# The depthwise convolution of a state-space block: products with pre-scaled weights on TensorE in place of multiply-adds on VectorE

## The chip, the cores and the metric

One core of one Trainium2 chip runs the whole program in one launch. The metric is device time in microseconds (us). The engines have queues of their own that run in order: TensorE (PE; its weight loads are shown as PEld), VectorE (DVE), ScalarE (ACT), GpSimd (POOL), and SyncE (SP), which issues nearly all DMAs. An instruction waits, with all that stands behind it on its queue, until what it reads is there and what it writes is free.

## The reference, cut to what matters

Layer 0 normalizes `x` (4 x 32 x 96 x 256, f32) in groups and runs two selective state-space blocks ("mamba") over it, one along the 96 time steps (way "t", sequences of length L = 96) and one along the 32 variables (way "d", L = 32). Each block computes, for a sequence of L tokens of 256 channels:

```python
xz = jnp.einsum('bld,ed->ble', x, in_w)
xi, z = jnp.split(xz, 2, axis=-1)                     # 512 channels each
xc = lax.conv_general_dilated(xi_nc, conv_w[:, None, :], (1,), [(D_CONV - 1, 0)],
                              feature_group_count=D_INNER)   # depthwise, causal, 4 taps
xc = jax.nn.silu(xc + conv_b[None, :, None]).transpose(0, 2, 1)
dbl = jnp.einsum('ble,fe->blf', xc, xproj_w)          # dt, B, C
# scan over l, 16 states per channel:
h = dA * h + dt_t[:, :, None] * B_t[:, None, :] * u_t[:, :, None]
y = jnp.einsum('bes,bs->be', h, C_t)
```

followed by a gate with silu(z) and an output product. Layer 1 is an additive attention over 3,072 tokens per batch entry and a graph-gated mixture of experts. The change touches only layer 0's convolution: for each channel, output l is the sum over j of `conv_w[3 - j] * xi[l - j]`, with nothing carried in from before the start of a sequence.

## The kernel before, in words

Layer 0 (`Layer0`) works in blocks of T = 384 tokens with 128 channels on the partitions, so a block has EC = 4 channel chunks e. Per batch entry there are 8 blocks of way t and 8 of way d. `run` writes the order by hand: t 0 to 7 of entry 0, then the first t block of entry 1, then d 0 to 7 of entry 0, and so on. The blocks 0 to 16 (`blk["lead"]`) run before anything else of the program does, since attention needs the finished rows of an entry; this is the stage that the change is in. From block 17 on, layer 0 runs beside attention, and ACT's large tanh sets the pace.

A block has a front (`front`: input product, convolution, xproj, time steps) and a back (`back`: decays, scans, products with C, gate), and the front of a block is issued beside the back of the one before. Both are lists of small jobs in 48 slots; `run` goes through the slots and issues, in each, first the back's scans and decays, then its inputs, outputs and sums, then the end of the block before, then the front's jobs. The order on PE, DVE, ACT and POOL is this order. SP's order is set by the framework's own scheduler.

The back walks 16 rounds of three slots (4 channel chunks x 4 groups of 4 states). A round has two scans of two states each. For each scan: ACT makes the decays `dA` (L470, two instructions, into one of two PSUM buffers that alternate), DVE makes `dB` (L483; every fourth one is made on POOL, L492), DVE scans (L503, `h`, four buffers), POOL multiplies `h` by C (L515), and PE sums the states with the identity as weights (L534, into `py`). After a chunk's 16 states DVE collects `py` (L541). Once per chunk PE makes the gate's product `pz` (L585).

The front's convolution, for chunk e, is `conv(e, s_mm, s_c0, s_c1, s_th, s_out)` at slots (13, 14, 15, 16, 18), (19, 20, 21, 22, 24), (22, 23, 24, 25, 27) and (25, 26, 27, 29, 30): PE makes `px`, two products of 128 x 128 weights with 384 columns (L296); ACT makes `acc = w[3] * px + bias` out of PSUM (L311, when the block before is a lead block); DVE adds three taps, each reading a shifted part of `px` (L302); ACT takes the tanh for the silu (L331); DVE finishes `xc` (L336). `px`, `pz`, `pd` (L349, xproj) and others share one PSUM buffer. In a round's terms, ACT's `acc` stands between the decays of one round and those of the next.

In way t POOL normalizes the block's input `xin` in slot 8 (L281); in way d ACT re-orders it into `xs`, so in a lead block the columns of one sequence are neighbours. The weights of the front (`self.wf`) are loaded at the start and again in slot 42 of the second-last block before the way changes (`fresh`), and `scale_front` rescales `xproj` on DVE there (L229). `uab` is a scratch tile that a front uses from slot 32 to 46.

Of the kernel before, what the change touches and what calls it, by code (L numbers as in the profile page):

```python
# [17 lines left out]
F32 = mybir.dt.float32  # L18
# [3 lines left out]
AF = mybir.ActivationFunctionType  # L22
# [4 lines left out]
P = 128  # L27
# [4 lines left out]
KC = C // P  # L32
# [101 lines left out]
class Layer0:  # L134
# [92 lines left out]
    def scale_front(self, t):  # L227
        nc, x = self.nc, t["xproj"]
        nc.vector.tensor_scalar(x, x, 0.5, None, ALU.mult)  # L229
        nc.vector.tensor_scalar(x[:, :, DR:DR + DS], x[:, :, DR:DR + DS], 0.5, None, ALU.mult)  # L230

    def scale_states(self, t):
        nc = self.nc
        nc.scalar.activation(t["A"], t["A"], AF.Exp)
        nc.vector.tensor_scalar(t["A"], t["A"], -1.0, None, ALU.mult)
        nc.vector.tensor_scalar(t["D"], t["D"], 0.5, None, ALU.mult)
# [5 lines left out]
    def front(self, blk, lead):  # L242
# [41 lines left out]
        elif alone:  # L284
            for k in range(KC):
                @at(11 + k)
                def _(k=k):
                    nc.scalar.copy(v["xs"][:, k, :].rearrange("p (s v) -> p s v", v=NV),
                                   v["xin"][:, k, :].rearrange("p (v s) -> p s v", s=ns))

        def conv(e, s_mm, s_c0, s_c1, s_th, s_out):
            @at(s_mm)
            def _():
                v["px"] = ps.tile([P, T], F32, tag="pp", name="px")
                for k in range(KC):
                    nc.tensor.matmul(v["px"], self.wf["in_x"][:, k, e * P:(e + 1) * P],  # L296
                                     blk["x"](k), start=(k == 0), stop=(k == KC - 1))

            def tap(j):
                a3 = v["acc"].rearrange("p (q l) -> p q l", l=L)  # L300
                p3 = v["px"].rearrange("p (q l) -> p q l", l=L)
                nc.vector.scalar_tensor_tensor(  # L302
                    a3[:, :, j:], p3[:, :, :L - j], self.wf["conv"][:, e, DCONV - 1 - j:DCONV - j],
                    a3[:, :, j:], ALU.mult, ALU.add)

            @at(s_c0)
            def _():
                v["acc"] = wk.tile([P, T], F32, tag="acc", name="acc", bufs=2)
                w, bias = self.wf["conv"][:, e, DCONV - 1:DCONV], self.wf["convb"][:, e:e + 1]
                if lead:  # L310
                    nc.scalar.activation(v["acc"], v["px"], AF.Identity, bias=bias, scale=w)  # L311
                else:
                    nc.vector.tensor_scalar(v["acc"], v["px"], w, bias, ALU.mult, ALU.add)
                    tap(1)

            @at(s_c1)
            def _():
                if lead:
                    tap(1)
                tap(2)  # L320
                tap(3)
                v["acc", e] = v["acc"]

            @at(s_th)
            def _():
                if alone:
                    blk["xc"][e] = self.ld.tile([P, T], F32, tag="xcl", name="xc", bufs=2 * EC)
                    xc = v["xt"] = self.ps_x.tile([P, 512], F32, tag="ex", name="xt")[:, :T]
                else:
                    xc = blk["xc"][e] = wk.tile([P, T], F32, tag="xc", name="xc", bufs=EC + 1)  # L330
                nc.scalar.activation(xc, v["acc", e], AF.Tanh, scale=0.5)  # L331

            @at(s_out)
            def _():
                xc = blk["xc"][e]
                nc.vector.scalar_tensor_tensor(xc, v["xt"] if alone else xc, 1.0, v["acc", e],  # L336
                                               ALU.add, ALU.mult)
# [410 lines left out]
    def run(self):  # L748

        order, NBLK = [], TOK // T
        for b in range(B):
            order += [(b, "t", i) for i in range(1 if b else 0, NBLK)]
            if b + 1 < B:
                order.append((b + 1, "t", 0))
            order += [(b, "d", i) for i in range(NBLK)]
        blocks = [{"b": b, "way": w, "i": i, "L": S if w == "t" else NV, "lead": n <= 2 * NBLK}
                  for n, (b, w, i) in enumerate(order)]

        FRONT, STATES = ("in_x", "conv", "convb", "xproj", "dt", "dtb"), ("A", "D", "in_z")

        def states_weights(blk):
            blk["w"] = {**self.weights(blk["way"], ("A", "D"), 2), **self.weights(blk["way"], ("in_z",))}
            self.scale_states(blk["w"])

        first = blocks[0]
        self.wf = self.weights(first["way"], FRONT)
        self.scale_front(self.wf)
        states_weights(first)  # L770

        def alone(*parts):
            for slot in range(48):
                fs = [f for part in parts for f in part.get(slot, [])]
                for f in fs:
                    f()
                if fs:
                    yield None
                    yield None

        yield from alone(self.front(first, True))
        left, ending = ({}, {}), {}
        rows = []
        for n, blk in enumerate(blocks):
            then = blocks[n + 1] if n + 1 < len(blocks) else None
            old = blocks[n - 1] if n else None

            fresh = then and n + 2 < len(blocks) and blocks[n + 2]["way"] != then["way"]
            if old is None or old["way"] != blk["way"]:
                if old and old["lead"] and not blk["lead"]:  # L790
                    self.dctx.close()
                    self.dA = self.decay_places(False)
                for t in self.dA:
                    for c0 in range(0, SB * T if blk["lead"] else T, T):
                        self.nc.vector.memset(
                            t[:, c0:c0 + T].rearrange("p (q l) -> p q l", l=blk["L"])[:, :, 0:1], 0.0)
            for name in ("bB", "bC"):
                for j in range(self.before(blk, name)):
                    if not left[1]:
                        self.broadcast(blk, name, j)  # L800

            breaks = then and (then["way"], then["i"]) == ("d", 0) and then["b"] == blk["b"]
            jobs, later = self.back(blk, None if breaks else then)
            ahead = self.front(then, blk["lead"]) if then and not breaks else {}
            for slot in range(48):
                self.slot = slot
                for f in left[0].get(slot, []) + jobs[0].get(slot, []):
                    f()
                yield None
                for part in (left[1], jobs[1], ending, ahead):  # L810
                    for f in part.get(slot, []):
                        f()
                if slot == 42 and old and "rows" in old:
                    rows = self.rows_keys(old)
                if rows:
                    rows.pop(0)()
                if slot == 12:
                    if old is None or old["way"] != blk["way"]:
                        blk["wo"] = self.weights(blk["way"], ("out",))
                        w = blk["wo"]["out"]  # L820
                        self.nc.vector.tensor_scalar(w, w, 0.5, None, ALU.mult)
                    else:
                        blk["wo"] = old["wo"]
                if slot == 42 and then:
                    if then["way"] == blk["way"]:
                        then["w"] = blk["w"]
                    else:
                        states_weights(then)
                    if fresh:
                        self.wf = self.weights(blocks[n + 2]["way"], FRONT)  # L830
                        self.scale_front(self.wf)
                if self.beside:
                    self.beside(slot, blk["way"] == "d" and blk["i"] >= min(PARTS))
                done = (old["b"], old["i"]) if old and slot == 11 and old["way"] == "d" else None
                if done == (0, NBLK - 1):
                    self.lctx.close()
                yield done
            left, ending = later, self.end(blk, bool(then and then["lead"]))
            if breaks:
                halves = 0  # L840
                for _ in chain(alone(*left, ending), alone(self.front(then, False))):
                    halves += 1
                    yield None
                left, ending = ({}, {}), {}
                for _ in range(-halves % (2 * NK_ATT)):
                    yield None
        yield from alone(*left, ending)
        yield blocks[-1]["b"], blocks[-1]["i"]
        yield None
# [1561 lines left out]
```

## Time and profile before

| | us |
|---|---|
| median of 3 runs | 14,503.21 (14,501.98 to 14,504.32) |
| the profiled execution, its own time | 14,508.64 |
| its span | 14,506.8 |
| PE, DVE, ACT, POOL busy in the span | 11,322 / 10,474 / 12,279 / 9,081 |

In the lead stage the profile's groups are: L302, the taps, 216 instructions of 0.58 to 0.61 us; L503, the scans, 1.75 us each, 32 per block; L483 0.95 us; L470 0.57 to 0.58 us; L515 1.8 us. One product in f32 shows as two matmul records. Times in the timeline count from the start of the span. In brackets stands how long an engine was idle before an instruction, and what released it.

### The profile page before, as it was taken

To read this page: it belongs to the slowest core of one execution; us is meant where nothing else is said; L and a number is where in the kernel's file an instruction comes from. 1 tells how busy PE (TensorE), PEld (TensorE's weight loads), DVE (VectorE), ACT (ScalarE), POOL (GpSimd) and SP (SyncE) were. 2 spreads that over 40 slices of the span, in tenths; PEclk is the share of its full clock that TensorE was granted. 3 is DMA by queue.
4 is the path that set the end of the run, shared out by engine and by line. 5 is a ranking of instruction groups with operands and counts; after the bars stand their busy time and mean duration, and the time that the engine had idled before them with its cause. 6 is when DMAs were issued, how large, how long until landed. Compare 5 with 4: busy or idle time off the path is not lost.

```text
span 14506.8 us, 224766 instructions
## 1 busy us (share of the span) xinstructions
PE 11322.4 (78%) x86704; PEld 5143.5 (35%) x86704; DVE 10473.8 (72%) x15217; ACT 12278.6 (85%) x9676; POOL 9080.5 (63%) x7108
## 2 busy tenths in 40 slices
PE   5777767777777777778887677788887788888888
PEld 2333322222232333333333233333333334443566
DVE  7888987787777877777777777757776785332376
ACT  4555569999999899999998899999999999999522
POOL 5777777777777667767776677747764003653373
PEclk8989978888888889989998899999989999999999
DMA  6778864445545444455554444435543100110233
GB/s 216 237 236 241 248 188 148 148 150 153 150 151 153 148 148 154 150 149 157 156 154 146 148 149 152 156 107 152 155 151 110 39 22 17 12 18 15 61 102 125
DMA packets 1199839, 1984.19 MB, mean 137 GB/s; under 512 B 418596, under 2 KB 646436, under 8 KB 1193636
## 3 DMA queue, kind: packets, MB, share of 16 engines
q1 hardware_dynamic: 1168036, 1963.77, 44.1%
q0 software_dynamic: 30720, 5.96, 0.9%
q8 instruction: 682, 11.17, 0.3%
q14 instruction: 401, 3.28, 0.1%
HBM read 1859.14 MB, written 110.18 MB: 136 GB/s over the span
## 4 chain that ended last, share of the span: by engine, by line


## 5 line engine op out<-in xcount | busy, mean ns | idle before, releaser
L1047 ACT ACTIVATE th<-krep,qsel 128x3072 f32<-128x3072 f32 x3072 | 8658.0, 2850 | 284.4 <-PE pe L1020 273.8
L1020 PE MATMUL pe<-th,wa_blk 128*32 128x384 f32 x49152 | 4933.7, 529 | 932.2 <-ACT pr L1115 691.0
L515 POOL TENSOR_TENSOR h<-h,bC 128x768 f32<-128x768 f32 x2048 | 3765.3, 1840 | 2769.4 <-DVE h L508 2198.2
L508 DVE TENSOR_TENSOR_SCAN h<-dA,dB 128x384 f32<-128x384 f32 x3008 | 2706.5, 941 | 895.9 <-ACT dA L470 673.8
L1020 PEld LDWEIGHTS pe<-th,wa_blk 128*32 128x32 f32 x49152 | 1468.5, 115 | 3408.8 <-issue 1877.1
L483 DVE TENSOR_TENSOR dB<-bB,dtu 128x768 f32<-128x768 f32 x1912 | 1809.9, 947 | 97.0 <-DMA bB<-bc 45.9
L522 POOL TENSOR_TENSOR h<-h 128x768 f32<-128x768 f32 x752 | 1413.5, 1880 | 53.6
L1133 PE MATMUL pv<-xn,pT 128*32 128x257 f32 x18432 | 1156.6, 401 | 216.7 <-DVE pT L1126 215.4
L470 ACT ACTIVATE dA<-dt,t_A 128x380 f32<-128x380 f32 x2048 | 1121.2, 571 | 230.2 <-DVE h L508 162.6
L534 PE MATMUL py<-h,ident 128*128 128x384 f32 x2176 | 930.0, 558 | 478.5 <-POOL h L515 370.4
L470 ACT ACTIVATE dA<-dt,d_A 128x372 f32<-128x372 f32 x2048 | 1107.2, 564 | 139.3 <-DVE h L508 91.8
L503 DVE TENSOR_TENSOR_SCAN h<-dA,dB 128x768 f32<-128x768 f32 x544 | 947.7, 1751 | 127.3 <-ACT dA L470 81.3
L1192 POOL TENSOR_SCALAR sf<-sel,f 128x32 f32<-128x32 f32 x384 | 137.3, 384 | 1239.3 <-ACT f L1188 1238.8
L1133 PEld LDWEIGHTS pv<-xn,pT 128*32 128x32 f32 x18432 | 598.4, 115 | 851.1 <-DVE pT L1126 373.7
L1108 DVE TENSOR_REDUCE nb<-pe 128x1 f32<-128x768 f32 x384 | 364.2, 948 | 729.0 <-PE pe L1020 697.1
L523 POOL TENSOR_TENSOR h<-h 128x384 f32<-128x384 f32 x752 | 790.4, 1051 | 59.0
L524 POOL TENSOR_TENSOR y<-y,h 128x384 f32<-128x384 f32 x752 | 777.1, 1033 | 59.0
L534 PEld LDWEIGHTS py<-h,ident 128*128 128x128 f32 x2176 | 420.2, 209 | 941.0 <-POOL h L515 583.5
L1124 PE MATMUL ptw<-ident,pr 128*128 128x128 f32 x2304 | 459.2, 314 | 306.4 <-DVE pT L1126 128.1
L1126 DVE COPY pT<-ptw 128x512 f32<-128x512 f32 (+1 forms) x768 | 417.6, 544 | 327.3 <-PE ptw L1124 315.4
L1276 POOL DMA_INDIRECT gd<-tab_a,di x480 | 498.3, 1038 | 159.2 <-issue 156.7
L1124 PEld LDWEIGHTS ptw<-ident,pr 128*128 128x128 f32 x2304 | 295.7, 159 | 770.9 <-issue 281.3
(329 smaller groups left out, 15071.9 us busy)
## 6 DMA issues: line engine op xcount, KB each, us to landing
bB<-bc SPq DMA_DIRECT2D x2048, 384.0 KB
bC<-bc SPq DMA_DIRECT2D x2048, 384.0 KB
x<-x SPq DMA_DIRECT2D x321, 128.0 KB
all<-kept SPq DMA_DIRECT2D x40, 1024.0 KB
kept<-ko SPq DMA_DIRECT2D x43, 512.0 KB
xt<-xn2T SPq DMA_DIRECT2D x41, 512.0 KB
qsel<-xn2T SPq DMA_DIRECT2D x75, 256.0 KB
kept<-eo SPq DMA_DIRECT2D x150, 128.0 KB
```

The lines of the kernel that those rows point to most:

```text
L470: nc.scalar.activation(inner(dA[:, s * T:(s + 1) * T] if alone else self.dA[s][:, :T]), inner(blk["dt"][:, e, :]), AF.Exp, scale=blk["w"][ ...
L483: nc.vector.tensor_tensor(dB, blk["bB"].pop(j), z["dtu"].unsqueeze(1).to_broadcast([P, SB, T]), ALU.mult)
L503: nc.vector.tensor_tensor_scan(flat(h), dA[:, :SB * T], flat(dB), 0.0, ALU.mult, ALU.add)
L508: nc.vector.tensor_tensor_scan(h[:, s, :], self.dA[s][:, :T], dB[:, s, :], 0.0, ALU.mult, ALU.add)
L515: nc.gpsimd.tensor_tensor(h, h, blk["bC"].pop(j), ALU.mult)
L522: nc.gpsimd.tensor_tensor(h0, h0, h1, ALU.add)
L523: nc.gpsimd.tensor_tensor(h0[:, 0, :], h0[:, 0, :], h0[:, 1, :], ALU.add)
L524: nc.gpsimd.tensor_tensor(y[e], y[e], h0[:, 0, :], ALU.add)
L534: nc.tensor.matmul(z["py"], self.ident, h[:, s, :], start=(i == 0), stop=(i == DS - 1))
L1020: nc.tensor.matmul(pe[q * QU:(q + 1) * QU, j, :KQ // 2], self.wa[:, k, :], th[:, c0:c0 + KQ // 2], start=(k == 0), stop=(k == NK - 1))
L1047: nc.scalar.activation(th, s["krep"], AF.Tanh, bias=s["qsel"][:, col:col + 1])
L1133: nc.tensor.matmul(pv[q * QU:(q + 1) * QU, :C + 1], pT[:, i, q * QU:(q + 1) * QU], s["xn"][:, q * NK + i, :], start=(i == 0), stop=(i == N ...
```

## The change

The convolution is linear in the input product, so the four taps can be put into the weights: `in_x4[:, j]` is `in_x` with each output channel multiplied by that channel's tap j. A convolution is then eight products, four taps times two chunks of 128 input channels, accumulated in one PSUM tile. The product of shift j writes the outputs from j on of each sequence and reads the inputs up to L - j, so its columns are 384 - 4j in way t (4 sequences of 96) and 384 - 12j in way d (12 of 32). ACT then only adds the bias, and DVE has no taps. `taps_load` brings `conv_w` flat to all 128 partitions (128 x 2,048 numbers, in the place of `uab`), `taps_make` makes `in_x4` with four DVE products of 128 x 1,024. This happens once in the prologue for way t, and for way d with the load in slot 47 of block 7 and the products in slot 6 of block 8. The fronts of blocks 0 to 16 take this way (`folded`); the front of block 17 and all later ones keep the old one. Taps and products of one convolution stay at the same slots.

```diff
+    def taps_load(self, t, way):
+        row = self.wide("taps")[:, :DI * DCONV]
+        flat = self.a[way]["conv_w"].rearrange("d k -> (d k)")
+        self.nc.sync.dma_start(row, flat.unsqueeze(0).to_broadcast([P, DI * DCONV]))
+        self.taps = t, row.rearrange("p (d k) -> p k d", k=DCONV)
+
+    def taps_make(self):
+        (t, row), self.taps = self.taps, None
+        t["in_x4"] = self.ld.tile([P, DCONV, KC, DI], F32, tag="inx4", name="inx4", bufs=1)
+        for j in range(DCONV):
+            self.nc.vector.tensor_tensor(t["in_x4"][:, j], t["in_x"],
+                                         row[:, j].unsqueeze(1).to_broadcast([P, KC, DI]), ALU.mult)
...
+        def folded():
+            return lead and "in_x4" in self.wf
...
                 v["px"] = ps.tile([P, T], F32, tag="pp", name="px")
+                if folded():
+                    parts = lambda t: t.rearrange("p (q l) -> p q l", l=L)
+                    for j in range(DCONV):
+                        for k in range(KC):
+                            nc.tensor.matmul(parts(v["px"])[:, :, j:],
+                                             self.wf["in_x4"][:, DCONV - 1 - j, k, e * P:(e + 1) * P],
+                                             parts(blk["x"](k))[:, :, :L - j],
+                                             start=(j == 0 and k == 0),
+                                             stop=(j == DCONV - 1 and k == KC - 1))
+                    return
...
-                if lead:
+                if folded():
+                    nc.scalar.activation(v["acc"], v["px"], AF.Identity, bias=bias)
+                elif lead:
                     nc.scalar.activation(v["acc"], v["px"], AF.Identity, bias=bias, scale=w)
...
-                if lead:
-                    tap(1)
-                tap(2)
-                tap(3)
+                for j in () if folded() else (1, 2, 3) if lead else (2, 3):
+                    tap(j)
...
         self.scale_front(self.wf)
+        self.taps_load(self.wf, first["way"])
+        self.taps_make()
...
+                if slot == 47 and fresh and blk["lead"] and blocks[n + 2]["lead"]:
+                    self.taps_load(self.wf, blocks[n + 2]["way"])
+                if slot == 6 and self.taps:
+                    self.taps_make()
```

## The prediction

> **What bounds the kernel now.** I read the page's busy shares, then the busy time in stretches of 100 us, because the change lives in the first stage alone: 17 blocks between 110 and 1,950 us of a 14,507 us span. Columns: stretch, length, then busy us and instruction count of PE, PEld, DVE, ACT, POOL, then the granted clock, the DMA share and GB/s. A t-block stretch and a d-block stretch:
>
> ```profile
> 560.00:660.00 100.00, 70.55 (x170) 33.35 (x171) 85.31 (x80) 51.86 (x94) 77.89 (x50) 0.90 0.79 243
> 1360.00:1460.00 100.00, 73.40 (x219) 38.43 (x219) 89.37 (x90) 60.06 (x119) 79.16 (x50) 0.94 0.82 241
> ```
>
> DVE is busiest (85 to 89%), and that is what the change relieves. But ACT, half idle, and PE are queues that run in order, so I asked next who waits for whom in the stage (waited us, times, longest):
>
> ```profile
> ACT acc L311 <- PE px L296: 214.2, 68, 9.3
> ...
> DVE h L503 <- ACT dA L470: 80.3, 85, 7.0
> ```
>
> ACT already stands at the convolution's first operation until PE has `px`, in nearly every one of the 72 convolutions, 3.1 us each. Behind it on ACT stand the decays `dA` of the next two scans, and DVE's longest loss is for `dA`. Last, the timeline of one convolution, the first of a d-block (start, duration, engine, operation, count, and the idle time before it):
>
> ```profile
> 1461.28 1.45 PE L296 MATMUL px<-xs,d_in_x 128*128 128x384 f32 x4
> 1462.59 1.76 DVE L503 TENSOR_TENSOR_SCAN h<-dA,dB 128x768 f32<-128x768 f32 x1
> 1462.77 0.67 ACT L311 ACTIVATE acc<-px,d_convb,d_conv 128x384 f32<-128x384 f32 x1 [3.14 <-PE px L296]
> 1463.34 2.27 ACT L470 ACTIVATE dA<-dt,d_A 128x372 f32<-128x372 f32 x4
> 1464.26 0.59 DVE L541 SCALAR_TENSOR_TENSOR y<-xc,d_D,py 128x384 f32<-128x384 f32 x1
> 1464.77 0.95 DVE L483 TENSOR_TENSOR dB<-bB,dtu 128x768 f32<-128x768 f32 x1
> 1465.00 1.53 PE L534 MATMUL py<-h,ident 128*128 128x384 f32 x4 [2.27 <-DVE y L541]
> 1465.63 1.84 DVE L302 SCALAR_TENSOR_TENSOR acc<-px,d_conv,acc 128x372 f32<-128x372 f32 x3
> 1466.26 1.81 POOL L492 TENSOR_TENSOR dB<-bB,dtus 128x768 f32<-128x768 f32 x1
> 1467.39 3.39 DVE L503 TENSOR_TENSOR_SCAN h<-dA,dB 128x768 f32<-128x768 f32 x2
> ```
>
> Each f32 product of 384 columns leaves two records, so x4 is two products. The chain reads: `px` done 1462.73, `acc` 1463.4, first `dA` pair 1464.5. DVE reaches its scan at 1467.39, 2.9 us after that pair: this is the slack that the longer `px` may use, and 1.84 us of it is the taps that go.
>
> **The change, part by part.**
>
> *Removed.* Three taps per convolution, 0.58 to 0.61 us each (mean by row), 1.84 to 1.90 us together. 17 fronts of four convolutions are folded: one alone in the prologue, eight of way t and eight of way d beside other blocks. The front of block 17 keeps the old path. In-stage that is 64 x 1.85 = 118 us of DVE.
>
> *Added on PE.* `px` becomes 16 records instead of 4. Records follow each other at 0.32 us (the 12-record row of 4.19 us, and 1.45 us for four with the last one's tail). For t the widths are 384, 380, 376, 372, so 16 x 0.315 = 5.04 us; for d 384, 372, 360, 348, so 4.9 us. With the tail 5.2 and 5.05, against 1.45. The shifted outputs are runs of 95 down to 29 elements; TensorE writing such runs into PSUM is not in this trace. Bounds: 0.315 us a record if runs cost nothing, and 2.92/4 = 0.73 us from the worst pattern shown, a moving operand read at a 48-byte step:
>
> ```profile
> 3324.39 2.92 PE L296 MATMUL px<-xin,d_in_x 128*128 128x384 f32 x4
> ```
>
> I take 0.315: runs of 29 and more neighbours are nearer to the plain rows than to single elements. The Trainium skill, SBUF — State Buffer, section "Door 1: The DMA port swizzle", speaks against the change here: it says that any non-contiguous access to PSUM slows matmuls significantly. It gives no factor; if the 12 shifted records went at the row's 0.73, `px` would take 10 us, 5 more per convolution, and the sum below would be about 320 us higher. No row of before can show it.
>
> *ACT.* `acc` stays, without the per-partition scale: 0.67 us now, 0.57 by the row of L383 (bias alone). I leave out that 0.1.
>
> *A d-block, put back together from the rows* (PE, ACT, DVE, POOL each in order). `px` 1461.28 to 1466.3; `acc` to 1466.95; first `dA` pair 1468.1; scan 1468.15, against 1467.39: +0.8 although the taps are gone. Behind `px` on PE stand the products that sum `h` (1465.00 in the rows, now 1466.2), then the gate product `pz`, which no longer waits for the taps and stays near its time. The next three convolutions come one per three slots, and there PE is the bound: between two `px` lie two sums of 1.28 us, so 5.05 + 2.56 = 7.6 us per round, where the rounds now take 7.2, 6.4 and 8.2 us. Carried on with the same durations, `px` starts at 1474.9, 1482.4, 1489.9 (now 1474.31, 1480.51, 1486.62), and the scan after the fourth at 1496.8 instead of 1494.3: +2.5 us. DVE has nothing left to give back, for it waits for `dA` in each round.
>
> *A t-block.* Here the first `px` has no slack, since PE gets to it late (POOL is behind after normalizing `xin`) and DVE stands at the tap for `acc`:
>
> ```profile
> 688.08 1.60 PE L296 MATMUL px<-xin,t_in_x 128*128 128x384 f32 x4
> ...
> 689.72 0.67 ACT L311 ACTIVATE acc<-px,t_convb,t_conv 128x384 f32<-128x384 f32 x1 [8.99 <-PE px L296]
> ...
> 690.42 1.90 DVE L302 SCALAR_TENSOR_TENSOR acc<-px,t_conv,acc 128x380 f32<-128x380 f32 x3 [0.62 <-ACT acc L311]
> 692.24 3.40 DVE L503 TENSOR_TENSOR_SCAN h<-dA,dB 128x768 f32<-128x768 f32 x2
> ```
>
> `px` to 693.25, `acc` to 693.95, `dA` 695.15, scan 695.15 against 692.24: +2.9. Then `px` at 701.9, 709.55, 717.2 (now 699.15, 705.35, 711.52), the following scans at 708.95, 716.55, 724.2 (now 704.66, 711.09, 719.27): +4.9 after the fourth. PE gets a little back, because it stays warm where it now runs a sum and `pz` at 2.90 us for four records: `pd` ends +4.7 late. I take +4.7.
>
> Blocks: 8 x 4.7 + 8 x 2.5 = +58 us. Afterwards every engine stands equally late and the rest of a block repeats the same pattern (the t-blocks' first scans lie 107.6 to 109.6 us apart), so nothing returns. Attention starts only after the stage, so the end moves by the same.
>
> *Prologue.* The taps of all 128 partitions are 128 x 8 KB = 1.05 MB, queued on SP among the loads of `xs`; at 262 GB/s (first 60 us) +4.0. Four products of 1,024 elements on DVE at L483's rate (0.95 us for 768, so 1.24) are 5.0 us, from 65.4 to 70.4, before PE can start, now 66.92: +3.4 (reading the taps at a step of four is not shown: up to twice that, +8.4). The chain of four convolutions and `pd` takes 25.5 us now (66.92 to 92.4); new: the first `px` half cold, 7.6, then three of 5.04, four `acc` of 0.67, tanh 0.5, xc 0.55, `pd` 2.75: 29.2, +3.7. Together +11.
>
> *Change of weights before the d blocks.* Another four products on DVE in block 8: +5 (to +10). Its 1.05 MB wait on SP for `uab`, read last in slot 46, and have seven slots, 15 us, to land: nothing, or some us if the broadcasts queued behind it on SP come late; their three and four buffers cover 10 us. And one gain: the program's SP queue now has the load of `d_xproj` eight broadcasts earlier. DVE stood 8.48 us for it at 975.10. I take -8.5 (bounds -8.5 and 0).
>
> Sum: 58 + 11 + 5 - 8.5 = +65 us. The profiled execution took 14,508.6 us, 5.4 above the median of three; against its own time that is 14,573, against the median 14,568.
>
> **The rivals.**
>
> *DVE's relief counts in full, the kernel gets faster.* For it: DVE is the busiest engine, and the row of DVE waiting for `dA` (80 us) is small. Then -118 + 11 + 5 - 8.5 = -110 us, 14,393. It needs ACT to pass `px` without delaying `dA`: it decides where `px` is below about 4.6 us in the three rounds (7.3 us, their mean now, less 2.56 + 0.1) and below 4.3 us in a d-block's first. Mine is 5.05, not far, so a half gain is possible; against it stand ACT's 68 waits.
>
> *Same.* If only the first convolution of each t-block lost (2.9 x 8 = 23) and the rest evened out: +23 + 7.5, about +30 us or less, which lies at the edge of 0.2% (29 us), what a measurement of this kernel can tell from none.
>
> *Shifted outputs are slow.* With 0.73 us a record: +65 + 64 x 5 = +385 us, 14,890.
>
> **How the numbers follow.** Slower as worked 0.70, its own range +30 to +130 us; slow shifted outputs 0.06; same 0.13; faster 0.11, mostly as half the gain. So slower 0.76, same 0.13, faster 0.11. The range leaves out the full gain and the slow outputs: 14,480 to 14,640.
>
> **What would show it.** Right: `px` groups of 16 records in about 5.1 us; ACT's wait for `px` near 214 + 64 x 3 = 400 us and more; DVE's wait for `dA` up from 80 to 200 us or more; DVE's share in 160 to 1,900 us down from 86 to about 79%; block distances of 113 us (t) and 110 (d). Wrong: `dA` waits unchanged and block distances near 101 us (the rival), or records of 0.6 us and over.

## The result and the profile after

The changed kernel takes 14,582.66 us (median of five runs, 14,576.89 to 14,586.24); the kernel before, run beside it, 14,501.98. The ratio is 1.0056, 95% interval 1.0044 to 1.0067: 81 us slower, where +65 was forecast. The profiled execution has a span of 14,584.4 us, 77.6 more than before.

Of these, 75 arise in the lead stage. From the first scan of one block to the first of the next, in the profiled execution of each kernel:

| us | before | after | |
|---|---|---|---|
| first scan of block 0 | 112.0 | 122.8 | +10.8 |
| blocks 0 to 6 (t), mean | 108.9 | 114.2 | +5.3 each |
| block 7 (t, last) | 115.0 | 112.8 | -2.2 |
| block 8 (first beside a d front) | 115.3 | 127.6 | +12.3 |
| block 9 | 115.8 | 118.0 | +2.2 |
| blocks 10 to 14 (d), mean | 107.35 | 109.9 | +2.6 each |
| block 15 | 108.0 | 110.2 | +2.2 |
| first scan of block 16 | 1,865.3 | 1,940.5 | +75.2 |
| from there to the end of the span | 12,641.5 | 12,643.9 | +2.4 |

The last row is the same work in every kernel here, and varies between 12,608 and 12,648 us over all the traces of this case: a total says less than the stage.

The same two stretches of the lead stage as in the prediction, with the same columns (stretch, length, busy us and count of PE, PEld, DVE, ACT, POOL, granted clock, DMA share, GB/s):

```profile
560.00:660.00 100.00, 78.82 (x221) 41.23 (x220) 75.27 (x64) 42.91 (x77) 77.25 (x49) 0.95 0.70 227
1360.00:1460.00 100.00, 82.14 (x253) 47.01 (x252) 81.65 (x79) 56.36 (x112) 75.46 (x47) 0.93 0.81 237
```

DVE did get its relief (85 to 75, 89 to 82). PE took the work on (71 to 79, 73 to 82), and no engine is above 83%: the stage has become one of waiting. Which wait, the view of waits between 112 and 1,935 us tells (us, times, longest):

```profile
ACT acc L339 <- PE px L317: 409.7, 64, 13.1
DVE h L531 <- ACT dA L498: 254.2, 145, 7.4
```

These two were 214 and 80 us. DVE lost 118 us of taps and waits 174 us longer for the decays. One stretch of the timeline shows how: rounds 4 to 7 of a t-block, counted from 0 (start, duration, engine, operation, count, and the idle time before it):

```profile
724.56 5.24 PE L317 MATMUL px<-xin,inx 128*128 128x384 f32 x16
...
729.84 0.58 ACT L339 ACTIVATE acc<-px,t_convb 128x384 f32<-128x384 f32 x1 [11.43 <-PE px L317]
730.32 2.30 ACT L498 ACTIVATE dA<-dt,t_A 128x380 f32<-128x380 f32 x4
...
731.59 3.40 DVE L531 TENSOR_TENSOR_SCAN h<-dA,dB 128x768 f32<-128x768 f32 x2 [5.36 <-ACT dA L498]
...
738.52 5.24 PE L317 MATMUL px<-xin,inx 128*128 128x384 f32 x16
...
743.60 2.74 PE L562 MATMUL py<-h,ident 128*128 128x384 f32 x8
...
743.80 0.58 ACT L339 ACTIVATE acc<-px,t_convb 128x384 f32<-128x384 f32 x1 [7.58 <-PE px L317]
744.28 2.30 ACT L498 ACTIVATE dA<-dt,t_A 128x380 f32<-128x380 f32 x4
...
745.56 3.40 DVE L531 TENSOR_TENSOR_SCAN h<-dA,dB 128x768 f32<-128x768 f32 x2 [3.26 <-ACT dA L498]
...
746.18 5.24 PE L317 MATMUL px<-xin,inx 128*128 128x384 f32 x16
```

ACT had nothing to do for 11.43 us, yet the decays `dA` of the next scans, which need nothing from `px`, stand behind `acc` on its queue; DVE in turn stands 5.36 us for them. From the second `px` on, PE goes `px` 5.24, sums 2.74, `px` 5.24, and so on (the rows overlap a little): 7.66 us from one `px` to the next. That is the round that the prediction built, 7.6 us.

The records of `px`, with their minimum, median and maximum in ns (a record overlaps the next one; 16 take 5.24 us in way t and 5.09 in way d):

```profile
L317 PE MATMUL px<-xin,inx x576: 473/482/977, 72.8 to 986.5; 128*128 128x384 f32 x48, 128*128 128x380 f32 x48, 128*128 128x376 f32 x48, 128*128 128x372 f32 x48
L317 PE MATMUL px<-xs,inx x512: 453/476/1008, 1073.1 to 1889.9; 128*128 128x384 f32 x43, 128*128 128x360 f32 x43, 128*128 128x348 f32 x43, 128*128 128x372 f32 x42
```

Before, with 384 columns in every record, the median was 486 ns. Writing the shifted outputs, in runs of 93 to 95 (t) and 29 to 31 (d) elements, cost nothing that these rows show.

Last the scaling of the weights, first in the prologue, then in block 8 (timeline):

```profile
64.58 9.44 POOL L296 TENSOR_SCALAR xin<-xin,gm,gr 128x384 f32<-128x384 f32 x2 [64.14 <-DVE t_xproj L229]
...
64.73 7.92 DVE L244 TENSOR_TENSOR inx<-t_in_x,taps 128x1024 f32<-128x1024 f32 x4
...
72.80 8.01 PE L317 MATMUL px<-xin,inx 128*128 128x384 f32 x16 [8.87 <-DVE inx L244]
...
1046.99 8.93 DVE L244 TENSOR_TENSOR inx<-d_in_x,taps 128x1024 f32<-128x1024 f32 x4
...
1048.79 10.13 SPq L461 DMA_DIRECT2D bB<-bc  x2
...
1055.83 1.76 DVE L531 TENSOR_TENSOR_SCAN h<-dA,dB 128x768 f32<-128x768 f32 x1
...
1064.61 5.64 SPq L280 DMA_DIRECT2D xin<-xt  x2
...
1072.22 0.85 ACT L303 COPY xs<-xin 128x384 f32<-128x384 f32 x1 [10.13 <-DMA xin<-xt]
```

Each product takes 1.95 to 3.23 us, not the 1.24 assumed, and POOL's two normalisations beside them take 9.44 us where they took 3.35. In block 8 the scans stand for 8.9 us: round 1 takes 14.5 us in place of 5.7. SP's queue, in order, holds a broadcast for 10.13 us, since its buffer comes free late, and the load of the next `xin` comes behind it; ACT waits 10.13 us for that. Most of this last wait is not new, for before the change ACT stood at the same place:

```profile
1018.67 0.86 ACT L288 COPY xs<-xin 128x384 f32<-128x384 f32 x1 [7.96 <-DMA xin<-xt]
```

The round that holds this wait grew only from 11.4 to 12.6 us.

### The profile page after: what moved, and what is told of

Same layout as the page of the kernel before. It is cut to its first block, busy times and chain, and to the rows that moved or that the text cites. A ratio compares the mean times of both kernels' runs of the same rounds, so it can differ in the third digit from the quotient of the medians.

```text
span 14584.4 us, 226136 instructions
## 1 busy us (share of the span) xinstructions
PE 11529.2 (79%) x87520; PEld 5304.1 (36%) x87520; DVE 10372.5 (71%) x15021; ACT 12267.6 (84%) x9676; POOL 9082.2 (62%) x7108
## 4 chain that ended last, share of the span: by engine, by line
ACT 40%; PE 27%; DVE 18%; issue 7%; POOL 5%; DMA 2%; SPq 1%; DVEq 0%; another core or an unknown queue 0%; POOLq 0%; ACTq 0%
ACT th L1081 28%; PE pe L1054 9%; ACT dA L498 6%; PE pv L1167 4%; DVE h L536 4%; DVE h L531 3%; PE px L317 2%; DVE dB L511 2%; POOL h L543 2%; PE po L1963 2%; PE py L562 2%; PE ph L1955 1%; ACT pr L1149 1%; PE pa L1711 1%; PE pz L613 1%
## 5 line engine op out<-in xcount | busy, mean ns | idle before, releaser
L562 PE MATMUL py<-h,ident 128*128 128x384 f32 x2176 | 891.7, 540 | 396.6 <-POOL h L543 357.4
```

The lines of the kernel that those rows point to most:

```text
L562: nc.tensor.matmul(z["py"], self.ident, h[:, s, :], start=(i == 0), stop=(i == DS - 1))
```

## The experiments

Theory: the loss is a matter of order. `px` is long, `acc` waits for it at the head of ACT's queue, the decays wait behind `acc`, and DVE's freed time becomes waiting. Rivals: DVE's taps were hidden all along; PE has simply become the bound; the loss lies in the scaling. The kernel before was measured again beside these runs; it took 14,482.88 us beside the first four, 14,495.43 beside the next two and 14,474.31 beside the last two, and each ratio and difference below goes by its own. The changed kernel was not run again, so what a run gains on it is the difference of two such differences. Block times come from one profiled execution of each kernel.

**The short product: what the taps' removal is worth without PE's price.** Only the products of shift 0 are made.

```diff
-                    for j in range(DCONV):
+                    for j in (0,):
...
-                                             stop=(j == DCONV - 1 and k == KC - 1))
+                                             stop=(k == KC - 1))
```

> The changed kernel with the products of shift 0 alone: px is 4 records as before, DVE has no taps, the loading and scaling of the weights stays. It leaves out three of the four taps of the convolution in the first 17 fronts. It asks what DVE's relief is worth when nothing is paid for it on PE. Theory (the long px, which holds up the decays on ACT, ate the relief): with px at 1.45 us the rounds of the convolutions fall from 7.3 to about 5.4 us, some 6 to 7 us per block, so about -90 to -110 us against before, minus and plus nothing for the prologue and the second scaling (+10, -8): 14,390 to 14,420 us. Rival (DVE's taps hid behind the wait for dA already, so nothing was to be had): within 25 us of before, 14,480 to 14,530.

14,441.53 us, ratio 0.9973 (0.9963 to 0.9983): 41 us faster, between the two. The t-blocks take 105.15 us and the d-blocks 104.2, so the full relief of 7.4 us per block is worth 3.8 and 3.2. Rounds 6 to 8, where three convolutions follow each other, shorten from 21.9 to 17.7 us, but then 0.7 us (0.4 in way d) goes in round 10 and, in way d, 1.0 in round 2. In round 10 ACT stands at `dbl` until PE has `pd`, and the decays of the next scan stand behind `dbl`. In the timeline:

```profile
1460.39 0.47 ACT L384 COPY dbl<-pd 48x384 f32<-48x384 f32 x1 [4.79 <-PE pd L377]
...
1462.03 1.76 DVE L531 TENSOR_TENSOR_SCAN h<-dA,dB 128x768 f32<-128x768 f32 x1 [1.40 <-ACT dA L498]
```

So the rival of the prediction, a gain of 110 us from DVE's relief, was not there to be had in this order: with `px` no longer at all than before the gain is 41 us, scaling included. Some 6 us more may hide in block 7, which takes 111.8 us: DVE stands 8.0 us there for `d_xproj`, as it did before the change (8.5) and does in no run with a long `px`.

**The long product with the taps kept.** The kernel before, with 16 records of the changed shapes from the unscaled weights (so it computes something else); no taps loaded, nothing scaled.

```diff
+                if lead and alone:
+                    parts = lambda t: t.rearrange("p (q l) -> p q l", l=L)
+                    for j in range(DCONV):
+                        for k in range(KC):
+                            nc.tensor.matmul(parts(v["px"])[:, :, j:],
+                                             self.wf["in_x"][:, k, e * P:(e + 1) * P],
...
```

> The kernel before with px as 16 records (the shifted shapes, unscaled weights) and the taps left on DVE; the convolution's output is another one, since px is the sum of shifted products. It asks what the long px costs alone, with no scaling and no relief. Theory (with px at 5.1 us the rounds are set by PE and by ACT's wait, and DVE's 1.85 us per convolution lie beside them): nearly the same loss in the blocks as the change has, +60 to +100 us with the prologue, 14,560 to 14,600. Rival (the relief counts in full and the long px costs what it ate, some 118 + 60 us): +160 to +200 us, 14,660 to 14,700.

14,596.28 us, ratio 1.0082 (1.0065 to 1.0099): 113 us slower, more than the 60 to 100 that I expected (the 14,560 to 14,600 named there count from 14,502) and far from the rival's 160 to 200. Blocks: 115.7 (t), 112.3 (d); the first scan comes 16.6 us later than before, since in the prologue the taps and the long `px` stand one behind the other. Against the changed kernel's 114.2 and 109.9, taking the taps away under the long `px` is worth 1.5 and 2.4 us per block, a fifth and a third of DVE's 7.4. The waits say where the taps went:

```profile
DVE acc L312 <- ACT acc L321: 106.8, 47, 4.3
...
ACT acc L321 <- PE px L299: 411.9, 63, 12.4
...
DVE h L513 <- ACT dA L480: 77.5, 81, 7.3
```

DVE here waits 107 us at the first tap; the changed kernel waits for the decays instead. While DVE stands at the tap, ACT makes the decays behind `acc`. So much of the time that the taps take here becomes waiting once they are gone: 254 us for the decays there, 107 and 78 us here.

**`acc` behind the decays.** The changed kernel, with `acc` one slot later, so that on ACT it follows the first pair of decays of the next round.

```diff
+        late = 1 if lead and alone else 0
-        conv(0, 13, 14, 15, 16, 18)
+        conv(0, 13, 14 + late, 15, 16, 18)
...
```

> The changed kernel with ACT's acc one slot later in the folded fronts beside other blocks and the first one: it then stands behind the first pair of decays of the next round and not ahead of it. PE's order is as it is. Theory of the order on ACT (what px delays is dA of the next scan, for acc stands ahead of it): about 1.5 to 2.5 us less per convolution, -60 to -130 us against the changed kernel, 14,450 to 14,520. Rival (PE's 7.6 us per round set the time, wherever acc stands): 14,570 to 14,590, as the changed kernel.

14,506.5 us, ratio 1.0016 (1.0006 to 1.0026): 24 us above the kernel before, so some 57 of the 81 us are gone, just under the 60 to 130 expected. t-blocks take 109.35 us (114.2), d-blocks 106.95 (109.9). Nothing was done but to change the order on one queue, so the order was the loss in the blocks. The waits:

```profile
ACT acc L339 <- PE px L317: 306.0, 63, 10.2
...
DVE h L532 <- ACT dA L499: 196.3, 143, 7.5
```

DVE still waits 196 us for decays, and no gain over the kernel before is left in a t-block. The next runs ask why.

**`acc` two slots later,** and the gate's product one slot later, since both use the same PSUM buffer (the tanh of the first three convolutions moves by one slot, too).

```diff
-        conv(0, 13, 14, 15, 16, 18)
+        conv(0, 13, 14 + 2 * late, 15 + late, 16 + late, 18)
...
-            g = 12 * e + (5 if e == EC - 1 and not blk["lead"] else 4)
+            g = 12 * e + (5 if e == EC - 1 or blk["lead"] else 4)
```

> As the run with acc one slot later, but two slots later, behind both pairs of decays of the next round, and the gate's product one slot later, since it shares the PSUM buffer. Theory of the order on ACT: no scan waits for px any more; DVE runs ahead of PE over the four buffers of h while the three long px go by, and PE makes up for it in the rounds without one: 7 to 12 us less per block than the changed kernel, 14,390 to 14,470. Rival (PE's rounds set the time): 14,570 to 14,590. If only part of the loss goes, the h buffers or the PE's backlog hold DVE, and the profile will show DVE waiting for py or h.

14,499.0 us, ratio 1.001 (1.0 to 1.0019). t-blocks 109.06, d-blocks 107.3 us: 5 and 2.6 us less than the changed kernel, but no better than one slot, and the 7 to 12 us that I expected did not come. The waits:

```profile
DVE h L532 <- ACT dA L499: 130.2, 117, 4.2
DVE y L570 <- PE py L563: 71.2, 34, 3.2
```

The wait for decays falls by another 66 us, yet DVE now waits 71 us for the sums of PE (33 before the change), and round 10 takes 8.6 us in place of 6.3, where ACT gets `pd` 6.9 us after the round's first scan (4.6 with `acc` one slot later). PE is late wherever DVE meets it: in rounds 6 to 9 of a t-block it is busy all the time (columns as in the stretches above):

```profile
707.60:734.45 26.85, 26.85 (x85) 15.92 (x84) 21.75 (x19) 12.82 (x24) 19.94 (x12) 1.00 0.71 229
```

**`px` in two halves,** one per chunk of 128 input channels, the first half one slot earlier (with `acc` one slot later).

```diff
+            if lead and alone:
+                @at(s_mm - 1)
+                def _():
+                    v["px"] = ps.tile([P, T], F32, tag="pp", name="px")
+                    half(0)
             @at(s_mm)
...
+                if lead and alone:
+                    half(1)
+                    return
```

> The run with acc one slot later (+0.16% on before), and px in two halves of eight records: the first 128 input channels one slot earlier, the other 128 at the old slot, so that one sum of h stands between them on PE. The whole computation is kept. It asks whether what is left of the loss is the sums of h that wait 5.2 us behind px. If so, the rounds with a px lose their remaining 1 to 2 us each: 2 to 4 us less per block than with acc later alone, 14,430 to 14,480 where before is 14,483. Rival (the total of PE's work in these rounds counts, or the next user of the shared PSUM buffer): no change against acc later alone, about 14,506.

14,514.75 us, ratio 1.0011 (1.0002 to 1.002). t-blocks 109.16, d-blocks 106.6 us, as without the split. The rival holds, and of its two forms the one on PE: it is the amount of PE's work, not its grain, for in rounds 6 to 9 of the same t-block PE leaves only 0.1 us in which it could have waited for the shared buffer:

```profile
707.83:734.72 26.89, 26.79 (x84) 15.53 (x82) 21.68 (x21) 12.09 (x25) 19.94 (x13) 1.00 0.71 233
```

**The scaling earlier, or spread.** The same, with the t weights scaled between the statistics of the prologue, and the four d products in four slots of block 8.

```diff
+            if b == 3:
+                for j in range(DCONV):
+                    self.taps_make(j)
...
-                if slot == 6 and self.taps:
-                    self.taps_make()
+                if slot in (5, 7, 9, 11) and self.taps:
+                    self.taps_make((slot - 5) // 2)
```

> As the run with px in halves, and the scaling of the weights taken off DVE's path: for way t its load goes before the second batch entry's statistics and its four products before the fourth's, where DVE waits for xs; for way d the four products go to slots 5, 7, 9 and 11 of block 8 instead of all into slot 6. Expected: the first scan of block 0 at 112 to 115 us instead of 121, block 8 some 3 to 6 us shorter, together 8 to 14 us less than the run with halves alone. If DVE's 2.0 us each are paid in full in block 8 wherever they stand, 7 to 9 us less.

14,511.66 us, ratio 1.0008 (0.9999 to 1.0017), 3 us less than the run with halves alone, where 8 to 14 were expected. In block 8 it works: 118.2 us in place of 122.2. In the prologue it gives nothing (first scan at 122.8 us):

```profile
51.18 7.61 DVE L252 TENSOR_TENSOR inx<-t_in_x,taps 128x1024 f32<-128x1024 f32 x4
...
65.80 1.88 DVE L196 BATCH_NORM_STATS2 gst<-xs 128x6 f32<-128x512 f32 x3 [3.09 <-DMA xs<-in_xT]
...
72.81 0.20 DVE L208 RECIPROCAL gr<-gr 128x8 f32<-128x8 f32 x1 [0.97 <-ACT gr L207]
73.13 3.35 POOL L304 TENSOR_SCALAR xin<-xin,gm,gr 128x384 f32<-128x384 f32 x2 [72.69 <-DVE t_xproj L235]
```

The products stand between DVE's statistics of `xs`; its two buffers come free later, so the last loads come later, DVE waits 3.09 us for one of them, and the statistics end at 72.81 us where they ended at 64.84. DVE was busy for only 32.35 of the first 60 us before, yet these gaps cannot be filled for nothing, since the loads that it waits for wait in turn for its statistics.

**The scaling beside block 0.** With `acc` one slot later; the front of block 0 keeps its taps on DVE, and the t weights are scaled in slots 5, 7, 9 and 11 of block 0, as the d weights in block 8.

```diff
-        self.taps_load(self.wf, first["way"])
-        self.taps_make()
         states_weights(first)
...
         yield from alone(self.front(first, True))
+        self.taps_load(self.wf, first["way"])
```

> The changed kernel with acc one slot later, and with the scaling of both ways' weights moved beside other work: the front of block 0 keeps its taps on DVE, the t weights are scaled in slots 5, 7, 9 and 11 of block 0, one product each, and the d weights in the same slots of block 8. Theory (the scaling is all that was left of the loss once acc had moved): first scan back at 112 us, block 0 about 4 us longer than the other t-blocks, block 8 at 118 us as when its products were spread before, t-blocks 109.2, d-blocks 106.6; in all -15 to +10 us against the kernel before. Rival: DVE has no room beside block 0 either and pays the four products in full, 8 us, and block 8 stays at 122 to 124: +10 to +25 us.

14,496.51 us, ratio 1.0018 (1.0009 to 1.0027). The first scan is back at 110.9 us and block 8 at 118.9, but block 0 takes 117.0, where it took 109.3 with `acc` later alone (107.6 before): most of the four products' 9.8 us (2.46 each in the median). The blocks 1 to 6 took 111.0 us in this run and not the 109.3 that they took with `acc` later alone, every second one some 2 us more; no run explains that. The rival holds for block 0, the theory for block 8; the total is no better than before.

**The second convolution and the gate's product change places,** so that PE has its long work more evenly.

```diff
-        conv(1, 19, 20 + late, 21, 22, 24)
+        conv(1, *((16, 18, 18, 19, 21) if late else (19, 20, 21, 22, 24)))
...
+            if e == 1 and alone and then and then["lead"]:
+                g += 3
             put(g, gate_product(e), 0 if blk["lead"] else 1)
```

> The kernel with the scaling moved beside other work, and also PE's long px spread more evenly: the second convolution goes from slots 19 to 24 to slots 16 to 21 and changes places with the gate's product of the second chunk (from slot 16 to 19), so that three px in a row no longer lie three slots apart without a pause. Theory (rounds 6 to 9 are PE's: 27.1 us busy of 27.5 in the kernel with acc later): t-blocks 107 to 108, d-blocks 105 to 106, in all 15 to 35 us less than the kernel without the swap. Rival (the four rounds were only as long as the rest of the chain, collecting y and the xproj product, needs; or PE lacks the time in round 4 and 5, where POOL's normalisation is late): no change within 8 us.

14,499.19 us, ratio 1.0016 (1.0006 to 1.0025). Blocks 1 to 6 take 109.2 us, as with `acc` later alone, and d-blocks 107.1: no gain. The rounds only exchange their time (round 6 takes 8.2 us in place of 5.7, round 7 4.6 in place of 6.0).

What all this amounts to is seen in one view, the busy time over rounds 6 to 9 of the same t-block, in the columns of the stretches above. Kernel before:

```profile
697.33:724.52 27.19, 19.77 (x48) 9.82 (x48) 26.53 (x29) 11.87 (x23) 20.04 (x13) 0.87 0.71 234
```

Changed kernel:

```profile
736.69:765.98 29.29, 27.39 (x85) 15.75 (x84) 21.53 (x21) 12.42 (x24) 19.90 (x13) 1.00 0.69 215
```

`acc` one slot later:

```profile
707.80:735.33 27.53, 27.12 (x84) 15.84 (x84) 21.57 (x21) 12.10 (x25) 19.88 (x13) 1.00 0.74 228
```

Short `px`:

```profile
672.32:695.50 23.18, 16.68 (x47) 8.35 (x47) 21.56 (x21) 11.83 (x23) 19.19 (x13) 1.00 0.83 262
```

Before, DVE was busy for 26.5 of 27.2 us. With the change it needs 21.5, and PE needs 27.1 to 27.4: the bound has gone from one engine to another of the same size. In the changed kernel the order on ACT adds 2 us to that; with the better order PE fills 27.1 of 27.5 us, at a granted clock of 1.00, so these rounds can only get shorter with fewer products in them. Over the whole of that t-block PE is busy for 84.9 of 109.2 us; whether the long products fit into rounds outside 4 to 9 was not tested. In a d-block PE is full from round 4 on: with `acc` later it is busy for 38.6 of the 39.6 us of rounds 4 to 9 (11.11 + 27.44 in 11.89 + 27.74). The short `px` shows DVE's own limit, 21.6 of 23.2 us.

No version here that computes the whole convolution beats the kernel before. With `acc` later and `px` in halves the blocks come out even with it (109.2 against 108.9 us in way t, 106.6 against 107.35 in way d). What remains is the prologue, 8.5 to 11.5 us longer where its products are made there, and the scaling in block 8, some 3 us or more; against these stand the 6 us or so that block 7 is shorter.

## Why the prediction was right, point by point

*The signs.* Those named for it came: `px` in 5.24 and 5.09 us, ACT's wait for it 410 us, DVE's wait for `dA` 254, DVE's share between 160 and 1,900 us down from 87 to 79%, and 114.2 and 109.9 us from block to block.

*Blocks (58 us forecast, 62 measured).* The t-blocks lost 5.3 us (4.7), the d-blocks 2.6 (2.5). They lost it where the working said: round 4, which holds the first `px`, is 2.5 us longer in way t (2.9) and 1.0 in way d (0.8), and rounds 6 to 9 together 2.2 and 1.8. With blocks 7 and 8 counted at these rates it is 37.0 + 5.3 + 2.5 + 2.2 + 12.9 + 2.2 = 62. The later `acc` shows the cause, for it takes back 4.9 and 3.0 us of these: the order on ACT. The runs after it show PE full right behind.

*Record price.* 16 records take 5.24 us in way t and 5.09 in way d with the tail (5.2 and 5.05 forecast). The working is looser than its result: 16 x 0.315 leaves the widths out, and with them 0.315 gives 5.0 and 4.8; the 5.04 and 4.9 come out at the 0.32 of the rows. The rival of slow shifted outputs fell. The Trainium skill, SBUF — State Buffer, section "Door 1: The DMA port swizzle", says that any non-contiguous access to PSUM slows matmuls significantly. Runs of 29 and more f32 elements showed no slowing here: 482 and 476 ns a record in the median, with 348 to 384 columns, against 486 with 384.

*Prologue (+11 forecast, +10.8 measured).* The sum is right by luck, for two terms missed. The taps' load was put at +4.0 and cost nothing: the statistics ended at 64.26 us, 64.84 before. The scaling was put at +3.4 and cost 5.9 (`px` at 72.80 in place of 66.92). From `px` to the end of `pd` it took 29.5 us (29.2 forecast, 25.5 before), and 0.9 more than before from there to the first scan.

*Change of weights (+5 forecast, +9.8 measured).* Block 8 grew by 12.3 us, of which 2.5 is the usual share. This is the term that was mis-sized most, 4.8 of the 10 us by which the stage was underestimated; the blocks are another 4. Four products at 1.24 us were worked out from the row of `dB`, which reads neighbours (0.95 us for 768 elements, 1.24 ns an element; in proportion 1,024 would be 1.27 us, which changes little); they read the taps at a step of four numbers and took 1.97 to 3.23 us, 8.93 together. The prediction had this as its upper bound ("to +10") and took the lower. The same section of that page says that SBUF is read in lines of 16 bytes and that a step to a new line with each element costs extra; a tap every 16 bytes is just that, and 1.9 ns an element against 1.24 for `dB` agrees with it, though no run here separated the step from the rest of the instruction.

*The load of `d_xproj` (-8.5 forecast, -7.5 measured).* Block 7 fell by 2.2 us where its neighbours grew by 5.3. Its round with the stall went from 14.4 to 6.6 us. The reason given was the right one, for the load stands behind 504 broadcasts on SP where it stood behind 512. But this is the scheduler's doing and not the new loads': with the short `px` the load was back behind 512 and the stall was there, and with the long `px` of the kernel before, which loads nothing new, it stood behind 502 and the stall was gone.

*The sum.* 62 + 10.8 + 9.8 - 7.5 = 75 us at block 16, 77.6 at the end of the profiled execution; 81 in the medians.

*The rival "DVE's relief counts in full".* Its condition was right in kind (ACT must pass `px` without delaying the decays) and its price was not: with a `px` of 1.45 us the gain is 41 us, not 110.

*Where my expectations of the runs failed.* I put the gain of the short `px` at twice what it was, and that of `acc` two slots later, `px` in halves, the earlier scaling, the changed places and, in part, the scaling beside block 0 too high. Mostly the reason was the same: I took one wait away and did not ask which engine was full right behind it. In the prologue it was another: I did not ask what the loads wait for. The long `px` with the taps kept cost more than I expected, in the blocks (6.8 and 4.9 us where the change costs 5.3 and 2.6) and in the prologue.

## What to carry to other kernels

Before work is moved off the busiest engine, add up for the tightest stretch, not for the stage, what the receiving engine will then need there; here it was 27 us in rounds of 27 us, so the best order could only come out even. Ask next which in-order queue waits for the moved work and what stands behind it there: an instruction that waits for the longer product belongs behind work that does not need it, which alone was worth 57 of the 81 us. And price the set-up of such a change by its own access pattern, at a place where the engine it runs on has a gap.

## What the runs showed of the hardware that I had not expected

- f32 products on DVE of 128 x 1,024 elements, with one operand read at a 16-byte step, took 1.95 to 1.99 us at the least (in every kernel that makes them, both ways), 1.9 ns an element.
- Beside them POOL's normalisation went from 3.35 us for two to 9.44, while DVE's four took 7.92 us, hardly more than the 7.61 they took alone. With the scaling elsewhere POOL was back at 3.35. That agrees with The Trainium skill, SBUF — State Buffer, section "Who interferes with whom", which says that a DVE instruction with two inputs in SBUF contends with a GpSimd instruction that reads SBUF. Spread over the slots of a block, beside POOL's products, the same DVE products took 2.46 us in the median and up to 2.95: there DVE loses as well.
- The granted clock in rounds 6 to 9 was 0.87 before and 1.00 with the long `px`, but also 1.00 with the short one, where PE's busy share was no higher than before (16.7 of 23.2 us against 19.8 of 27.2). So the share alone does not decide it.
